# Graph network on one core: the first group's side loads stand ahead of its messages, and these are fetched by SyncE and ScalarE in turn

## The chip, the cores and the metric

The kernel runs on one core of one Trainium2 chip. The metric is the device time in microseconds (us); lower is better. PE is TensorE, DVE is VectorE, ACT is ScalarE, POOL is GpSimd and SP is SyncE. SP computes nothing: it issues DMA transfers and waits. ACT computes, and has a DMA queue of its own as well.

## The reference

Two graph layers act on 6250 nodes of 160 features (64 scalars and 32 vectors of 3) and 100000 edges, sorted by their target. Cut to what matters:

```python
h = relu(layernorm(x))
m = tensor_product(h[dst], edge_attr) + linear(h[dst])     # one message per edge
a = segment_sum(m, src, N)                                 # summed at the nodes
x = x + h + tensor_product(h, a) + linear(h)               # the node update
h = relu(layernorm(x))
m = tensor_product(h[src], edge_attr) * sigmoid(edge_attr16 @ W + b)
x = x + linear(h + segment_sum(m, dst, N))
```

The change lies between the first `segment_sum` and the node update of the first layer, whose tensor product multiplies every pair of features of `h` and `a` by weights.

## The kernel before, in words

There are three stages. **Scatter** makes the messages of the first layer, 128 edges at a time. GpSimd writes each to its place in the DRAM tensor `msgs` (L563), so that messages of 25 neighbouring nodes, a bin, lie together. It also writes the nodes' normalised features to DRAM, in the layouts `hT`, `hX` and `hV`. **Update** sums the messages per node and makes the node update. **Windows** does the second layer.

The update treats the nodes in 13 groups of up to 500. A group has 20 bins, in five *quads* of four bins. For a group it needs:

- the *messages*: `fetch(k)` (L683) loads quad k into a tile `urec`. Each bin is one DMA of 322 KB (128 partitions by 4 rows of 161 floats). Its first row is a value that the device has computed, so that a `value_load` reads it from `start_i` into a register first. There are three `urec` buffers. `sums` (L696) turns a quad into sums: ACT negates the node numbers (`rl`, L706), DVE makes a selection matrix (`uhot`, L711 and L715), PE multiplies (L734), and ACT copies the result (`ag`, L740 and L742). After each quad, the fetch of the quad three further on is called. When all five are done, PE puts the sums into the layout of the products (L755), and ACT copies them into `a` (L751).
- the *sides*: `loads` (L759) brings the group's own features as twelve DMAs: `x0` (L762), `x1` (L764), four for `x1k` (L767), and three each for `x3` and `v3` (L773 and L774).
- `xb` (L815), four DMAs at a time, which POOL multiplies by `a` (L822).

The products follow: PE, DVE and POOL work through a stream of 32 steps per group, `first` and `second`, beginning with the product at L833. While they work on a group, the sums of the next are made between their steps.

The orders of PE, DVE, ACT and POOL are as written (`manual_schedule`). SP's order is laid out by the scheduler of the tile framework: a transfer stands where its buffers and its source allow it, in the order of the calls where they don't decide. `issue_after` keeps the fetches in order. A fetch of `msgs` waits until all of the scatter has landed.

The loads of SP and ACT are told done by eight completion semaphores, which the framework gives out in turn to both queues. An instruction that is given a used one waits for the load that had it before.

Of the kernel before, what the change touches and what calls it, by code (L numbers as in the profile page):

```python
# [36 lines left out]
CAP = 512  # L37
# [19 lines left out]
def gnn_kernel(ctx: ExitStack, tc: tile.TileContext, a: dict, out: bass.AP):  # L57
    nc = tc.nc
# [3 lines left out]
    E = ET * P  # L62
# [16 lines left out]
    msgs = dram.tile([E + CAP, F + 1], F32, name="msgs")  # L79
# [66 lines left out]
    start_i = const.tile([1, NBIN], I32, name="start_i")  # L146
# [143 lines left out]
    def clear(tab):  # L290

        flat = tab.rearrange("(p r) f -> p (r f)", p=P)
        for lo in range(0, flat.shape[1], 400):
            hi = min(lo + 400, flat.shape[1])
            nc.scalar.dma_start(flat[:, lo:hi], zero[:, :hi - lo])
            yield
# [326 lines left out]
    def update():  # L623
# [3 lines left out]
        with ExitStack() as s:  # L627
# [47 lines left out]
            nc.gpsimd.memset(mv, 0.0)  # L675
            eps = wp.tile([P, 1], F32, name="eps")
            nc.gpsimd.memset(eps, EPS)
            last = []

            quads = [(g, q) for g, (_, n) in enumerate(groups) for q in range(0, n // BW, 4)]  # L680
            got = {}

            def fetch(k):  # L683

                if k >= len(quads):
                    return
                g, q = quads[k]
                b0, nq = groups[g][0] // BW + q, min(4, groups[g][1] // BW - q)
                got[g, q] = recs.tile([P, 4, 4, F + 1], F32, name="urec")
                for b in range(nq):  # L690
                    with tc.issue_after(last[-1]) if last else nullcontext():
                        at = nc.sync.value_load(start_i[0:1, b0 + b:b0 + b + 1], min_val=0, max_val=E)
                    last.append(nc.sync.dma_start(got[g, q][:, b], msgs[bass.ds(at, CAP), :]
                                                  .rearrange("(p i) f -> p i f", i=4)).ins)

            def sums(g, a):  # L696

# [29 lines left out]
                for j, (q, nq) in enumerate(qs):  # L727
                    if g == 0 and j + 1 < len(qs):
                        yield from ones(*qs[j + 1])
                    p = pt.tile([P, 4 * P], F32, name="ptr")  # L730
                    rec, hot = got.pop((g, q)), hots.pop(0)
                    for i in range(4):
                        for b in range(nq):
                            nc.tensor.matmul(p[32 * b:32 * b + 32, :F], hot[:, b, i], rec[:, b, i, 0:F],  # L734
                                             start=i == 0, stop=i == 3, tile_position=(0, 32 * b))
                    fetch(quads.index((g, q)) + 3)
                    yield
                    w = 32 * nq
                    ag = pool.tile([P, 4, P], F32, name="ag", bufs=5)
                    nc.scalar.copy(ag[:w, 0].rearrange("p (i f) -> p i f", i=2),  # L740
                                   p[:w, None, 0:M0].to_broadcast([w, 2, M0]))
                    nc.scalar.copy(ag[:w, 1:].rearrange("p k (i f) -> p k i f", i=4),  # L742
                                   p[:w, M0:F].rearrange("p (k f) -> p k f", k=3)[:, :, None]
                                   .to_broadcast([w, 3, 4, M1]))
                    ags.append(ag)
                    if g and j + 1 < len(qs):
                        yield from ones(*qs[j + 1])
                    yield
# [200 lines left out]
            eng = mybir.EngineType  # L949
            with tc.manual_schedule(engines={eng.PE, eng.DVE, eng.Activation, eng.Pool}):  # L950
                R = len(plan)
                stream = [(g, kind, c) for g in range(len(groups)) for kind, c in plan]
                rows = [(i, g, c[1]) for i, (g, kind, c) in enumerate(stream) if kind == "v" and c[0] == 0]
                early = list(rows)
                queue, backs, end = [], [], object()
                clears = itertools.chain(*(clear(t) for t in agg))

                def pop():
                    _, _, grp, item = queue.pop(0)
                    grp.second(*item)  # L960
                    if grp.done():
                        backs.append(grp.back())
                        next(backs[-1])

                for k in range(3):
                    fetch(k)
                gs = {0: Group(0)}
                for _ in gs[0].sums:
                    pass
                for i, (g, kind, c) in enumerate(stream):  # L970
                    r = i % R
                    if r % 8 == 6:
                        next(clears, end)
                    if r == 3 and g + 1 < len(groups):
                        gs[g + 1] = Group(g + 1)
                    while rows and rows[0][0] <= i + 7 and rows[0][1] in gs:
                        gs[rows[0][1]].repeat(rows.pop(0)[2])
                    while early and early[0][0] <= i + 2 and early[0][1] == g:
                        gs[g].ahead(early.pop(0)[2])
                    if r == 2:  # L980
                        while queue and queue[0][2] is not gs[g]:
                            pop()
                    for item in gs[g].first(kind, c):
                        queue.append((g, i + later[kind], gs[g], item))
                    if r == 2:
                        gs[g].begin()
                    queue.sort(key=lambda q: q[:2])
                    while queue and queue[0][1] <= i and queue[0][2].begun:
                        pop()

                    for _ in range((2, 2, 0, 1)[r % 4] if r >= 3 and g + 1 < len(groups) else 0):
                        next(gs[g + 1].sums, end)
                    for _ in range((1, 2, 0, 1)[r % 4]):
                        while backs and next(backs[0], end) is end:
                            backs.pop(0)
                    if r == R - 1 and g + 1 < len(groups):
                        for _ in gs[g + 1].sums:
                            pass
                while queue:
                    pop()  # L1000
                for t in backs + [clears]:
                    for _ in t:
                        pass
# [677 lines left out]
    with tc.tile_pool(name="early", bufs=1) as pool:  # L1681
        e = early(pool)
        update()
        windows(e)
# [93 lines left out]
```

## Time and profile before

The median of three executions is 3754.78 us (3748.99 to 3765.18). The profiled execution took 3762.7 us, with a span of 3760.6 us in the records.

| stretch of the span (us) | what runs | PE busy | DVE busy | POOL busy | clock | DMA share |
|---|---|---|---|---|---|---|
| 0 to 60 | the bins, first tables | 29.29 | 44.64 | 16.16 | 0.86 | 0.61 |
| 60 to 1350 | scatter | 696.26 | 686.03 | 767.42 | 0.70 | 0.53 |
| 1350 to 1412 | from scatter to update | 19.10 | 14.97 | 14.05 | 0.56 | 0.81 |
| 1412 to 2330 | update | 849.65 | 705.16 | 680.41 | 0.99 | 0.54 |
| 2330 to 3761 | windows | 817.34 | 767.70 | 741.26 | 0.63 | 0.47 |

Busy times are in us of the stretch. The clock is the TensorE clock that the throttle granted, as a part of full speed; the DMA share is the mean busy share of the core's 16 DMA engines. In the timelines a line begins with its start and its duration; `SPq` and `ACTq` are transfers issued on the queues of SP and ACT, shown at their issue and not at their landing. `L693` is a line of the kernel.

### The profile page before, as it was taken

The page shows a single profiled execution, that of the slowest core. Times are in us where ns is not written, and L with a number is a line of the kernel's source. Part 1 is how long each engine was busy: PE and PEld are TensorE (multiplying, and loading weights), DVE is VectorE, ACT ScalarE, POOL GpSimd, SP SyncE. Part 2 cuts the span into 40 slices and gives each one's busy share as a digit, 9 for nine tenths or more (in the row PEclk, how much of TensorE's full clock was granted, in tenths as well). Part 3 has the DMA queues.
Part 4 walks back from the last instruction along what each step waited for, and adds up shares of the span by engine and source line. Part 5 has one row for each costly group of instructions (what it writes and reads, how often), then busy time and mean ns, then how long its engine had stood idle before and what let it go on. Part 6 is the DMA issues. An engine that isn't in the chain of part 4 may idle for free. (4 is left out here: it accounts for less than half of the span.)

```text
span 3760.6 us, 47934 instructions
## 1 busy us (share of the span) xinstructions
PE 2411.6 (64%) x12112; PEld 1273.7 (34%) x12112; DVE 2218.5 (59%) x4577; ACT 1547.0 (41%) x5126; POOL 2219.3 (59%) x1864
## 2 busy tenths in 40 slices
PE   5555565565544439999999998455655565655655
PEld 3433343343333323333333333132323333332323
DVE  7665555555444427777777775455555556555554
ACT  4554444554444424544453441333434333433433
POOL 4655555555666537777777775655555555555552
PEclk8677767776666659999999999566666666666666
DMA  6655555555444456665565532445444454445442
GB/s 176 172 162 162 151 160 174 153 171 153 135 132 130 135 178 179 181 181 159 173 182 176 165 116 70 130 131 147 133 136 132 135 141 139 132 134 146 134 132 71
DMA packets 346121, 554.56 MB, mean 147 GB/s; under 512 B 63954, under 2 KB 245168, under 8 KB 339947
## 3 DMA queue, kind: packets, MB, share of 16 engines
q1 hardware_dynamic: 229160, 288.49, 27.7%
q0 software_dynamic: 87584, 218.31, 19.9%
q10 hardware_dynamic: 29091, 44.61, 3.6%
q8 instruction: 99, 1.62, 0.2%
q14 instruction: 187, 1.53, 0.1%
HBM read 418.16 MB, written 133.04 MB: 147 GB/s over the span
## 5 line engine op out<-in xcount | busy, mean ns | idle before, releaser
L563 POOL DMA_INDIRECT msgs<-rec,pos_i x782 | 782.5, 1001 | 568.2 <-issue 223.9
L1060 POOL DMA_INDIRECT wgot<-T,src_i x782 | 741.3, 948 | 636.0 <-issue 423.7
L543 PE MATMUL rank<-seen,every 128*128 128x256 f16 x782 | 261.2, 334 | 449.3 <-ACT junk L556 296.5
L556 ACT ACTIVATE junk<-rank,off 128x256 bf16<-128x256 f32 x782 | 373.2, 477 | 403.5 <-remote 284.5
L545 PE MATMUL pmsg<-tw,d 120*128 120x160 f32 x1564 | 463.4, 387 | 79.8 <-issue 68.8
L1079 PE MATMUL wgate<-wrad,wblk 97*128 97x480 f32 x522 | 378.6, 858 | 175.0 <-issue 133.3
L855 DVE TENSOR_TENSOR pr<-y,a 128x1000 f32<-128x1000 f32 (+1 forms) x312 | 352.7, 1153 | 132.7 <-PE y L852 131.9
L840 POOL TENSOR_TENSOR pr<-pr 128x1500 f32<-128x1500 f32 (+1 forms) x104 | 338.1, 3251 | 149.1 <-DVE pr L837 149.1
L1097 DVE TENSOR_TENSOR whot<-lane,wbank 128x192 f32<-128x192 f32 x131 | 45.9, 350 | 619.4 <-ACT wbank L1205 550.1
L1216 PE MATMUL wbank<-wms,whot 128*32 128x160 f32 x1564 | 255.7, 411 | 213.6 <-ACT wo L1220 104.5
L545 PEld LDWEIGHTS pmsg<-tw,d 120*128 120x128 f32 x1564 | 317.0, 251 | 147.4 <-issue 93.4
L1091 ACT ACTIVATE wm<-wgot,wattr 128x160 f32<-128x160 f32 x782 | 311.1, 398 | 34.9 <-DMA wgot<-T,src_i 12.6
L560 DVE CAST pos_i<-pos 128x4 int32<-128x4 f32 x196 | 42.4, 216 | 419.1 <-ACT junk L556 347.5
L1216 PEld LDWEIGHTS wbank<-wms,whot 128*32 128x32 f32 x1564 | 146.4, 144 | 405.9 <-ACT wo L1220 137.5
L1094 ACT ACTIVATE wsg<-wgate 128x480 f32<-128x480 f32 x259 | 137.5, 566 | 352.7 <-remote 187.7
L860 POOL TENSOR_TENSOR ppr<-ppr,pr 128x1000 f32<-128x1000 f32 (+1 forms) x104 | 232.0, 2231 | 79.5 <-DVE pr L855 77.1
L544 PEld LDWEIGHTS <-upto 128*128 128x128 bf16 x782 | 91.6, 117 | 541.5 <-issue 499.3
L544 PE MATMUL rank<-hot,upto 128*128 128x256 bf16 x782 | 262.2, 335 | 0.5 <-DVE hot L528 0.5
L531 DVE TENSOR_TENSOR seen<-seen,hot 128x256 f16<-128x256 f16 x782 | 230.5, 295 | 45.5 <-DVE hot L528 7.6
L528 DVE TENSOR_SCALAR hot<-binb,qb 128x256 bf16<-128x256 bf16 x782 | 242.7, 310 | 0.0
L1079 PEld LDWEIGHTS wgate<-wrad,wblk 97*128 97x128 f32 x522 | 131.2, 285 | 314.2 <-issue 239.6
L1115 DVE TENSOR_TENSOR wm<-wm,wtb 128x384 f32<-128x384 f32 (+1 forms) x393 | 221.8, 564 | 13.5
(215 smaller groups left out, 4430.2 us busy)
## 6 DMA issues: line engine op xcount, KB each, us to landing
urec<-msgs SPq DMA_DIRECT2D x250, 322.0 KB
attb<-in_attr SPq DMA_DIRECT2D x48, 960.0 KB
tw<-T0s SPq DMA_DIRECT2D x391, 75.0 KB
xb<-hT SPq DMA_DIRECT2D x192, 125.0 KB
dstb<-in_dstrow SPq DMA_DIRECT2D x48, 480.0 KB
T0s<-tt ACTq DMA_DIRECT2D x11, 1200.0 KB
msgs<-rec,pos_i POOLq DMA_INDIRECT x782
wgot<-T,src_i POOLq DMA_INDIRECT x782
```

Of the source, the lines that this page charges most:

```text
L528: nc.vector.tensor_scalar(hot, binb, qb[:, t:t + 1], None, op0=OP.is_equal)
L543: nc.tensor.matmul(rank[:, j % 2], every, before, start=True, stop=False)
L544: nc.tensor.matmul(rank[:, j % 2], upto, hot, start=False, stop=True)
L545: nc.tensor.matmul(prs[-1][:, j % 2, :F], ds[j // WP][:, j % WP], tws[j // WP], start=True, stop=True)
L556: nc.scalar.activation(junk, rank, AF.Relu, bias=off, accum_out=pos[:, j:j + 1])
L563: nc.gpsimd.indirect_dma_start(out=views[(t0 + j) % NV][:, :], out_offset=bass.IndirectOffsetOnAxis(ap=pos_i[:, j:j + 1], axis=0), in_=rec ...
L840: nc.gpsimd.tensor_tensor(prs[0], prs[0], prs[1], op=OP.add)
L855: nc.vector.tensor_tensor(pr[:, :, :n], y[:, :, :n], a[:, j, None, :n].to_broadcast([P, 2, n]), op=OP.mult)
L1060: nc.gpsimd.indirect_dma_start(out=got[u][:, i], out_offset=None, in_=T1[:, :], in_offset=bass.IndirectOffsetOnAxis(ap=src_i[:, t0 + i:t0 ...
L1079: nc.tensor.matmul(p[:, :n], blocks[u // CH][:, u % CH], rad[:, lo * F:lo * F + n], start=True, stop=True)
L1091: nc.scalar.activation(m[:, b, j:j + F], g[:, i, oS1:oS1 + F], AF.Copy, scale=attr(u)[:, i, 0:1])
L1216: nc.tensor.matmul(state["acc"][j:j + WN], hot[:, i], ms[:, i], start=t0 + i == w * WT, stop=t0 + i == end, tile_position=(0, j))
```

## The change

The construction of the first group, which issues its sides, is moved ahead of the first three fetches. And in group 0 the bins of a quad are fetched by SP and ACT in turn: bins 0 and 2 by SP, bins 1 and 3 by ACT, each with a `value_load` on its own engine. Each queue keeps its own order (`last` is now a table by queue). The other groups are fetched by SP alone, as before. Behind the change, line numbers are higher by up to 3.

```diff
-            last = []
+            last = {}
...
                 for b in range(nq):
-                    with tc.issue_after(last[-1]) if last else nullcontext():
-                        at = nc.sync.value_load(start_i[0:1, b0 + b:b0 + b + 1], min_val=0, max_val=E)
-                    last.append(nc.sync.dma_start(got[g, q][:, b], msgs[bass.ds(at, CAP), :]
-                                                  .rearrange("(p i) f -> p i f", i=4)).ins)
+
+                    o = b % 2 if g == 0 else 0
+                    eng = (nc.sync, nc.scalar)[o]
+                    with tc.issue_after(last[o]) if o in last else nullcontext():
+                        at = eng.value_load(start_i[0:1, b0 + b:b0 + b + 1], min_val=0, max_val=E)
+                    last[o] = eng.dma_start(got[g, q][:, b], msgs[bass.ds(at, CAP), :]
+                                            .rearrange("(p i) f -> p i f", i=4)).ins
...
+                gs = {0: Group(0)}
                 for k in range(3):
                     fetch(k)
-                gs = {0: Group(0)}
                 for _ in gs[0].sums:
                     pass
```

## The prediction

> **What bounds the kernel now.** I read first the busy time by stage, to see what a delay at the hand-over from scatter to update is worth. The columns are the stretch in us, its length, busy us of PE, weight loads, DVE, ACT and POOL, the granted clock, the DMA share and GB/s.
>
> ```profile
> 1350.00:1412.00 62.00, 19.10 (x204) 14.49 (x204) 14.97 (x30) 9.36 (x31) 14.05 (x21) 0.56 0.81 242
> 1412.00:2330.00 918.00, 849.65 (x5500) 315.49 (x5498) 705.16 (x680) 390.29 (x1418) 680.41 (x260) 0.99 0.54 158
> ```
>
> From 1412 to 2330 the update keeps PE busy for 849.65 of 918 us at clock 0.99: PE bounds it, and an earlier start of its first product is an earlier end. In the 62 us before, every engine is mostly idle while the DMA share is 0.81: this is the only place that the change touches. Next, the timeline there: start, duration, engine, and in brackets the idle time before and what ended it. ACT's first instruction on each quad (`rl`, L706) waits for the quad's messages:
>
> ```profile
> 1377.74 0.23 ACT L706 ACTIVATE rl<-urec 128x16 f32<-128x16 f32 x1 [23.40 <-DMA urec<-msgs]
> ...
> 1382.49 0.23 ACT L706 ACTIVATE rl<-urec 128x16 f32<-128x16 f32 x1 [4.53 <-DMA urec<-msgs]
> ...
> 1400.68 0.23 ACT L706 ACTIVATE rl<-urec 128x16 f32<-128x16 f32 x1 [3.75 <-DMA urec<-msgs]
> ...
> 1411.19 0.68 PE L833 MATMUL y<-x,w_f 64*128 64x500 f32 x1
> ```
>
> The five quads of group 0 are met at 1377.74, 1382.49, 1388.29, 1396.17 and 1400.68 (the rows of quads 2 and 3, alike, are left out); the first product of the update follows the last by 10.5 us. So the arrival of quad 4 is the number to follow. Third, the issues of SP, one by one:
>
> ```profile
> 1370.32 0.37 SPq L693 DMA_DIRECT2D urec<-msgs  x1
> ...
> 1374.07 0.33 SPq L693 DMA_DIRECT2D urec<-msgs  x1
> ...
> 1383.34 0.89 SPq L767 DMA_DIRECT2D x1k<-hT  x2
> ...
> 1388.13 0.30 SPq L774 DMA_DIRECT2D v<-hV  x1
> 1389.27 0.36 SPq L693 DMA_DIRECT2D urec<-msgs  x1
> ```
>
> The first fetch is issued as soon as the scatter has landed. Twelve stand there, 1.11 us apart; then eight side loads hold SP from 1383.34 to 1389.27, and only after them come the eight fetches of quads 3 and 4. Last, how full the DMA is:
>
> ```profile
> 1370.00:1372.00 2.00, 0.00 (x0) 0.00 (x0) 0.40 (x2) 0.00 (x0) 0.00 (x0) 0.50 0.32 49
> ...
> 1376.00:1378.00 2.00, 0.00 (x0) 0.00 (x0) 0.00 (x0) 0.23 (x1) 0.00 (x0) 0.50 1.00 312
> ...
> 1384.00:1386.00 2.00, 2.00 (x32) 1.34 (x32) 0.00 (x0) 0.00 (x0) 0.00 (x0) 0.50 0.95 305
> ...
> 1388.00:1390.00 2.00, 0.04 (x4) 0.07 (x6) 1.12 (x2) 0.76 (x3) 0.00 (x0) 0.50 0.54 126
> ```
>
> One fetch is 322 KB, 0.330 MB; at 1.11 us that is 297 GB/s, and the rows show 312 and 305 at shares of 1.00 and 0.95 (289 to 304 at about 0.9 in those between). SP's issuing and the DMA are almost equally fast. The holes are at the start (0.32) and where the sides stood (0.54).
>
> **The change, part by part.** *Sides first.* In the built order of SP four of the twelve side loads (x0, x1, two of x1k) already stand ahead of the messages; the change moves the other eight: two x1k of 187.5 KB and six of 62.5 KB, 0.77 MB. What leaves the path: SP's stretch from 1383.34 to 1389.27, less one ordinary 1.11 us step, about 5 us. Where they go: after the x1k issue at 1362.33. The DMA is 0.73 to 0.99 busy there until 1368 with scatter and weights, then 0.37 and 0.32 until 1372, so some 2.6 us of empty DMA hold them; 0.77 MB at 250 GB/s (estimate, between the 205 of 1386 to 1388, where they ran, and 305) is 3.1 us. Left over, or lost by the scatter's tail: 0 to 1 us, taken as 0, since the last of them run beside ACT's first fetch, where the DMA is not yet full.
>
> *What is queued behind them.* SP's and ACT's loads take eight completion semaphores in turn, and an issue waits until the load that last held its semaphore has landed. In the built order one moved x1k thus waits for the second weight load, which landed by 1367.47 (its scaling on DVE starts then), the third x3 waits for w_n, issued at 1367.08, and **the eighth moved load, the last v3, waits for ACT's first fetch to land**. All of SP's own fetches stand behind that v3. So SP cannot begin at 1370.3. ACT does: its first fetch waits for the scatter, 1370.3. Issue to landing is 3.67 us for the fourth fetch before (1374.07 to 1377.74), 3.98 for the eighth, 3.5 for the last two quads; I take 3.5: landing at 1373.8, SP's v3 there, SP's first fetch at 1374.3, four later than now. Ends of this unknown: 3.5, and 4.6 (ACT's 256 KB weight load, 1362.84 to 1367.47 beside others).
>
> *Two queues.* Ten of group 0's twenty fetches go to ACT, six of them ahead of its first `rl`. Each is a register load, a check and a DMA. ACT has nothing else then: its idle time before the first `rl` is 23.4 us, so six times 1.11 us cost nothing; without that cover 6.7. ACT's third fetch reuses the semaphore of its second (issued 1371.5, landed 1375.0). The bytes: two fetches from ACT until about 1373.7, a hole until 1375.3 (SP's issue plus 1 us, as now from 1370.32 to 1371.4), then eighteen fetches with more than enough issuers. A rule is weighed here. The Trainium skill, "DMA: Bandwidth & Descriptors", section "Issuing engines are not separate DMA queues", says that transfers started by different engines interleave on the same 16 DMA engines and that a second issuer only saves issuing time. By it the second queue gives no bandwidth and the eighteen go at the rate of the fullest plain row, 305 GB/s: 1.08 us each, 19.4 us. The same page's table of specifications puts a core's share of HBM at about 358 GB/s: 0.92 us each, 16.6 us. No row here shows fetches above 312, so I take 19.4, and keep 16.6 as an end. 1375.3 + 19.4 = 1394.7, and 1.3 from the last byte to `rl` (3.5 less 1.1 and 1.1): **quad 4 at 1396.0 instead of 1400.68**.
>
> *Do the three buffers allow it?* Quad 3 reuses quad 0's buffer. Quad 0's two halves now share the DMA with others and land about three and a half fetches after 1375.3: 1380.4, 2.7 later than now. Its matmuls end 4.0 later (1377.74 to 1381.79 now): 1384.4. The ten fetches under way last until 1386.1, and new bytes flow 1.1 us after an issue, so the slack is 0.6 us and no hole opens; ACT's half of quad 3 stands behind `rl` of quad 1, which needs only quad 1 (1384.7). For quad 4 the same sum leaves about as little. I allow up to 2 us for holes at the pessimistic end.
>
> *The rest.* ACT loads its first start register during the scatter, at the sixteenth send. The DVE cast it needs ends at 145.76, ACT arrives at 146.4, and ACT idles 2.82 us soon after, waiting for PE: 0 us, at most 1.1 without that cover. POOL's first product needs xb, whose last three loads stay behind group 1's fetches on SP. Now SP comes late: quad 4's matmuls end at 1404.7, xb is issued from 1411.71 and POOL starts at 1417.65. Afterwards these matmuls end at 1400.0; four fetches and three xb on SP take 6.4 us, and 3.3 to land give 1409.7: eight earlier, not a new bound. From the next group on the orders on SP and ACT are the same.
>
> Sum: -4.7 us at quad 4, carried by PE to the end. Ends: with 16.6 us for the fetches -7.5; with 4.6 us to land, 1.14 us per fetch (289 GB/s) and 2 us of holes, 1.1 + 1.1 + 2 given back, -0.5. The profiled execution took 3762.7 (span 3760.6 and 2.1 around it) and becomes 3758.0; that execution stands 7.9 above the median of 3754.8, so I forecast **3750.1**.
>
> **The rivals.** *More than that*: the hold by ACT's first fetch is hidden, because ACT alone fills the DMA for those us, and two queues beat 305 GB/s. Twenty fetches without a hole at 0.92 to 1.0 us from 1371.4, and 1.3, give 1391.1 to 1392.7: 8.0 to 9.6 us less, about 3746. Against it: 1.00 share at 312 GB/s with one queue.
>
> *It does not do what it says*: only eight of twelve loads move, SP is still held by the last of them, and quad 0 lands later by what quad 4 gains. If PE's start then hangs on something else, it is 3755. For it: the 0.6 us of slack; against it: 10.5 us from quad 4 to the first product are pure work on PE and ACT.
>
> *Slower*: the semaphore chain. Place: SP's last v3 behind ACT's first fetch; price: each us by which that fetch lands late delays ten SP fetches, thereby quad 0, its buffer, and quads 3 and 4, one for one once the 0.6 us of slack are gone. It decides when the landing takes 3.5 + 0.6 + 4.7 = 8.8 us; at 12 it gives 3758. Against it: on a quiet DMA the fourth fetch landed after 3.67.
>
> **How the numbers follow.** About 0.5% (18.8 us) is what a measurement of this kernel can tell from no change; the three executions already lie 16 us apart. The forecast (3747 to 3754): 0.63. More: 0.15. Nothing: 0.13. Slower by 1 to 6 us: 0.07. The rest, 0.02, is something unseen. None of the cases reaches 18.8 us either way; only the spread of executions or something unseen does: faster 0.03, same 0.93, slower 0.04. Range: from 3746 of the first rival to 3758 of the last, widened by half the spread of the executions at the lower end and a third at the upper: 3740 to 3762.
>
> **What would show it.** In the trace after: the eight side loads issued between 1362 and 1374; ACT's first fetch near 1370.3 and SP's first some four us behind it; quad 0 later than 1377.74 while quad 4 is earlier, near 1396; the hole at 1388 to 1390 gone; the first product near 1406.5; the update's length unchanged near 918 us. The prediction is wrong if SP's first fetch comes more than 6 us after ACT's, if the bytes stop between quads 2 and 3, or if the update's length takes the gain back.

## The result

The changed kernel takes 3759.02 us (median of 20 runs, 3748.68 to 3773.05), the kernel before 3756.39 us in the same comparison (20 runs, 3743.17 to 3771.61): a ratio of 1.0002, 95% interval 0.9993 to 1.0011, which is no change that can be measured. The forecast was 3750.1 us, in a range of 3740 to 3762. The executions of either kernel lie 24 to 28 us apart, so the 4.7 us that the prediction spoke of do not show in these times, and have to be looked for in the traces, stage by stage. The profiled execution has a span of 3749.6 us (before: 3760.6).

The busy time by stage first, in the changed kernel, for the same two stretches as before (length, busy us of PE, weight loads, DVE, ACT and POOL, clock, DMA share, GB/s):

```profile
1350.00:1412.00 62.00, 24.84 (x213) 16.55 (x213) 20.25 (x32) 10.82 (x38) 15.60 (x19) 0.56 0.79 259
1412.00:2330.00 918.00, 848.88 (x5503) 315.96 (x5501) 699.78 (x681) 389.86 (x1412) 675.12 (x259) 0.99 0.54 158
```

The update is as full as it was: PE 848.88 us of 918 against 849.65, at clock 0.99. The change shows only in the 62 us before it, where more of the work lies ahead of 1412. Next the timeline of the changed kernel there: `rl` of quads 0, 1, 3 and 4, and the first product.

```profile
1377.06 0.23 ACT L709 ACTIVATE rl<-urec 128x16 f32<-128x16 f32 x1 [26.91 <-DMA urec<-msgs]
1380.10 0.23 ACT L709 ACTIVATE rl<-urec 128x16 f32<-128x16 f32 x1 [2.81 <-DMA urec<-msgs]
...
1387.24 0.23 ACT L709 ACTIVATE rl<-urec 128x16 f32<-128x16 f32 x1 [0.98 <-DMA urec<-msgs]
...
1391.95 0.23 ACT L709 ACTIVATE rl<-urec 128x16 f32<-128x16 f32 x1 [3.90 <-DMA urec<-msgs]
...
1403.58 0.68 PE L836 MATMUL y<-x,w_f 64*128 64x500 f32 x1
```

The clock of the trace starts with the execution, so these are to be read from the first fetch, which stood at 1370.32 before and stands at 1365.94 now. Quad 0 comes 11.12 us after it (before 7.42), quad 4 at 26.01 (before 30.36), the first product at 37.64 (before 40.87). The gain is 4.35 us at quad 4 and 3.2 at the first product; 1.1 us are lost between the two. The issues of ACT and SP at the hand-over, in the timeline of the changed kernel:

```profile
1365.94 0.38 ACTq L696 DMA_DIRECT2D urec<-msgs  x1
1369.54 0.30 SPq L777 DMA_DIRECT2D v<-hV  x1
1370.37 0.37 SPq L696 DMA_DIRECT2D urec<-msgs  x1
```

The last moved side load is issued 3.60 us after ACT's first fetch, and SP's own first fetch 4.43 us after it. And the DMA in 2-us stretches of the changed kernel (columns as above):

```profile
1370.00:1372.00 2.00, 0.00 (x0) 0.00 (x0) 0.00 (x0) 0.00 (x0) 0.00 (x0) 0.50 0.38 80
...
1376.00:1378.00 2.00, 0.00 (x0) 0.00 (x0) 0.61 (x1) 0.23 (x1) 0.00 (x0) 0.50 1.03 388
1378.00:1380.00 2.00, 1.25 (x20) 1.12 (x24) 0.50 (x2) 0.00 (x0) 0.00 (x0) 0.50 1.03 402
...
1382.00:1384.00 2.00, 1.93 (x32) 1.02 (x24) 0.42 (x1) 0.78 (x3) 0.00 (x0) 0.50 0.83 200
1384.00:1386.00 2.00, 1.01 (x16) 0.91 (x20) 0.70 (x2) 0.39 (x2) 0.00 (x0) 0.50 1.05 412
```

With two queues the rows reach 388 to 412 GB/s, where one had 312 at the most in the rows shown. (The share adds up the times of the packets that start in a row, so it can pass 1.) But there are two holes, 80 GB/s while SP is held, and 200 GB/s from 1382 to 1384. They take back most of what the fast rows gain.

### The profile page after: what moved, and what is told of

Its sections match the earlier page's. It is cut to its first block, busy times and chain, and to the rows that moved or that the text cites. A ratio compares the mean times of both kernels' runs of the same rounds, so it can differ in the third digit from the quotient of the medians.

```text
span 3749.6 us, 47940 instructions
## 1 busy us (share of the span) xinstructions
PE 2401.2 (64%) x12112; PEld 1270.6 (34%) x12112; DVE 2214.9 (59%) x4577; ACT 1546.4 (41%) x5126; POOL 2215.5 (59%) x1864
## 4 chain that ended last, share of the span: by engine, by line
PE 30%; another core or an unknown queue 22%; DVE 17%; ACT 13%; issue 10%; DMA 5%; SPq 1%; POOL 1%; ACTq 1%; DVEq 0%; POOLq 0%
PE out L871 5%; DVE pr L840 4%; ACT junk L556 3%; ACT wm L1094 3%; PE pmsg L545 3%; PE wbank L1219 3%; PE wgate L1082 2%; PE y L855 2%; PE wbank L1151 2%; PE y L836 2%; DVE wtb L1108 2%; PE rank L544 2%; PE rank L543 2%; DVE wm L1118 1%
## 5 line engine op out<-in xcount | busy, mean ns | idle before, releaser
L1082 PE MATMUL wgate<-wrad,wblk 97*128 97x480 f32 x522 | 370.0, 841 | 178.2 <-issue 137.6
L1118 DVE TENSOR_TENSOR wm<-wm,wtb 128x384 f32<-128x384 f32 (+1 forms) x393 | 221.7, 564 | 13.4
```

Source lines behind the costliest of these rows:

```text
L1082: nc.tensor.matmul(p[:, :n], blocks[u // CH][:, u % CH], rad[:, lo * F:lo * F + n], start=True, stop=True)
L1118: nc.vector.tensor_tensor(mv[:, :, :, 0:M0], mv[:, :, :, 0:M0], tb[:, :nt, k].rearrange("p (b t) w -> p b t w", b=h), op=OP.add)
```

## The experiments

Two theories were set against each other first. *Spread*: 3 to 5 us are gained at the hand-over, and chance in the long stages hides them. *Given back*: a later stage returns them. Each row of the table is one trace, its last column a ratio from all executions. The last scatter write is counted from its issue. Kernels 1 to 4 ran on one chip, 5 to 8 on a second, whose granted clock is higher (mean 0.82 to 0.84 in the traces against 0.75; the kernel before takes 3075.72 us there), 9 to 12 on a third (3724.77 us). Each is compared with the kernel before on its own chip.

| kernel | last scatter write to first fetch | first fetch to quad 0 | to quad 4 | to first product | last scatter write to first product | first product to first gather of the windows | ratio to before (95%) |
|---|---|---|---|---|---|---|---|
| before | 4.79 | 7.42 | 30.36 | 40.87 | 45.7 | 933.5 | |
| changed | 5.33 | 11.12 | 26.01 | 37.64 | 43.0 | 932.8 | 1.0002 (0.9993 to 1.0011) |
| 1 before again | 5.02 | 7.23 | 30.09 | 40.0 | 45.0 | 931.2 | 0.9985 (0.9974 to 0.9996) |
| 2 changed again | 11.00 | 13.16 | 28.93 | 39.3 | 50.3 | 930.9 | 0.9976 (0.9964 to 0.9988) |
| 3 sides only | 5.11 | 7.25 | 25.67 | 35.4 | 40.5 | 930.9 | 0.9990 (0.9977 to 1.0002) |
| 4 queues only | 4.85 | 8.27 | 25.63 | 34.7 | 39.5 | 927.6 | 0.9990 (0.9976 to 1.0004) |
| 5 quad 0 by SP | 2.87 | 10.41 | 26.14 | 35.6 | 38.5 | 930.1 | 0.9988 (0.9980 to 0.9995) |
| 6 late start | 2.71 | 10.02 | 25.98 | 50.1 | 52.8 | 939.4 | 1.0072 (1.0059 to 1.0085) |
| 7 changed, third | 3.65 | 10.99 | 24.98 | 36.7 | 40.4 | 934.9 | 0.9988 (0.9981 to 0.9996) |
| 8 queues, again | 2.65 | 8.36 | 27.13 | 35.6 | 38.2 | 928.6 | 0.9986 (0.9978 to 0.9993) |
| 9 changed, four buffers | 6.34 | 12.13 | 24.45 | 33.4 | 39.8 | 933.0 | 0.9994 (0.9973 to 1.0014) |
| 10 quad 0 by SP, four buffers | 6.24 | 11.54 | 22.75 | 30.7 | 36.9 | 930.0 | 0.9992 (0.9967 to 1.0017) |
| 11 changed, small pools | 11.31 | 12.24 | 26.24 | 36.6 | 47.9 | 927.2 | 0.9981 (0.9961 to 1.0000) |
| 12 before, control | 2.96 | 7.28 | 29.37 | 38.6 | 41.6 | 933.9 | 1.0007 (0.9990 to 1.0024) |

**1 and 2: both kernels once more.** No edit. Expected of the kernel before:

> The kernel before, unchanged, profiled a second time, to learn how far the intervals repeat. Theory A (the hand-over is shorter by about 3 us and this is lost in the spread between executions): from the first fetch to quad 4 30.4 us again within 0.5, quad 4 to the first product 10.5, first product to first gather of the windows 933.5 within 1, while the time up to the first fetch (1370.3) and from the first gather to the end (1415.9) move by 3 us or more. Theory B (the change gives its gain back in the scatter or the windows): those two long parts repeat within 1 us, so that a change of 3 us in them would be an effect. Ratio 1.000.

and of the changed one:

> The changed kernel again. Theory A: first fetch to quad 4 26.0 within 0.5, quad 4 to first product 11.6, first product to first gather 933 within 1; the long parts before and behind come out anywhere within 5 us of the kernel before. Theory B: the scatter or the windows come out longer than in the kernel before by 3 us, in both of its profiles. Ratio by A 0.9990, by B 1.000; the spread of executions of 7 us leaves the ratio alone unable to tell them.

The unchanged kernel measured 3760.48 us and came out at 0.9985 of itself, with an interval that leaves out 1 although nothing was changed; a ratio within 0.15% of 1 therefore says nothing here. The changed kernel measured 3756.48 us, 4.0 under the control beside it, where the first comparison had it 2.6 over. Of the two theories, *spread* is the one that the traces bear out: the first fetch stands at 1370.3 and 1385.3 us in two traces of the same unchanged kernel, and the part from the first gather to the end, 1415.8 and 1412.8 us before, is 1413.1 and 1414.8 us in the changed kernel, so that no later stage is seen to return a gain. The part between them, from the first product to the first gather, was expected to repeat within 1 us and did not: it is 933.5 and 931.2 us before, 932.8 and 930.9 changed.

In the second trace of the changed kernel quad 4 is at 28.93, the worst of the four traces of this hand-over and later than expected; still 1.2 us better than the 30.09 of the control. What was not expected is the row ahead of it: the first fetch comes 11.00 us after the last scatter write. The timeline of this second trace, POOL's last scatter write and ACT's queue:

```profile
1361.34 1.55 POOL L563 DMA_INDIRECT msgs<-rec,pos_i  x1 [0.30 <-issue]
...
1371.18 0.59 ACTq L92 DMA_DIRECT2D w_n<-in_n  x1
1372.34 0.38 ACTq L696 DMA_DIRECT2D urec<-msgs  x1
```

ACT's fetch stands behind seven loads of weights on ACT, and in this execution their issue ends last: the fetch follows the last of them by 1.16 us. SP is late for the same reason. The chain of this trace, of which these are consecutive long pieces, leads from a load for the windows (`wattr`) to a weight on ACT's queue (`w_flu`), which was given the same semaphore, and from there to a side load on SP:

```profile
1363.12 6.28 DMA wattr<-in_attr
1369.42 4.83 DMA w_flu<-in_flu
1374.27 0.30 SPq L777
```

SP's first fetch follows at 1377.12, after four more side loads. ACT's first fetch had landed before the last of these was issued (it took 2.7 to 3.6 us in the traces where a side load did wait for it), so here it held nothing back. Counted from the last scatter write, the first product comes after 50.3 us, against 45.7 and 45.0 in the two traces of the kernel before.

**3 and 4: each part alone.** Sides ahead, all fetches by SP:

```diff
-                    o = b % 2 if g == 0 else 0
+                    o = 0
```

> One part of the change alone: the sides ahead of the messages, all fetches on SP. If the hold of SP behind ScalarE's first fetch costs what I think, this part alone is as good as the whole change: no hold, first SP fetch as soon as the scatter has landed, twenty fetches at 1.11 us, quad 4 at 1.11 x 19 + 0.5 + 3.5 = 25.1 us after the first fetch (whole change 26.0, before 30.4). If the two queues carry the gain instead, quad 4 stays near 28 or later. Ratio 0.9987 by the first, 0.9995 by the second.

Two queues, the sides left where they were:

```diff
-                gs = {0: Group(0)}
                 for k in range(3):
                     fetch(k)
+                gs = {0: Group(0)}
```

> The other part alone: fetches in turn on SP and ScalarE, the eight sides still behind the first three quads on SP. No hold of SP's first fetch. If two queues move the messages faster than 305 GB/s, quad 0 lands 5.5 to 6.5 us after the first fetch (before 7.4), quad 2 about 13 (18.0), and the sides still delay SP's half of quads 3 and 4: quad 4 at 25 to 27. If the second queue brings nothing, quad 4 at 29 to 30. Ratio 0.9988 by the first, 0.9998 by the second.

Each part alone brings quad 4 to the same place as both together (25.67, 25.63, and 26.01 or 28.93), and the first product earlier than both together: 35.4 and 34.7 against 37.6 and 39.3. The parts don't add up. With the sides alone, the fetches leave SP almost without a pause, the first sixteen within 17.41 us, and quad 4 is bound by issuing (25.1 us expected). With the queues alone quad 4 came as expected, but quad 0 at 8.27 us (5.5 to 6.5 expected) and quad 2 at 17.39 (about 13). The times, 3758.75 and 3759.81 us, lie with the control's.

A part of the 2 to 3 us by which the single changes lead goes with PE's clock. The layout matmuls between quad 4 and the first product (L758), in the changed kernel and then with the sides alone (min/median/max ns, first and last start):

```profile
L758 PE MATMUL ptr<-quad,ag x40: 275/421/536, 1395.9 to 1403.4; 128*128 128x100 f32 x40
```

```profile
L758 PE MATMUL ptr<-quad,ag x40: 275/275/536, 1400.3 to 1405.8; 128*128 128x100 f32 x40
```

The same forty matmuls take a median of 421 ns in one and 275 in the other, and 7.5 against 5.5 us from the first to the last. In the changed kernel the granted clock stands at 0.50 until 36 us after the first fetch; with the sides alone it is at 1.00 from 32 us on. What raises it earlier was not tried, so the cause is open.

**5: without the hold.** Quad 0 by SP alone; in this built order no side load waits for a fetch of ACT.

```diff
-                    o = b % 2 if g == 0 else 0
+                    o = b % 2 if g == 0 and q else 0
```

> The changed kernel, but quad 0 is fetched by SP alone; quads 1 to 4 alternate as before. No side load then stands behind a fetch of ACT, so the hold of SP is gone. Theory A (the hold of SP's last v3 is what eats the second queue's gain: 4.4 and 4.8 us in the two traces of the changed kernel, whose quad 0 came 11.1 and 13.2 us after the first fetch against 7.2 to 7.4 before): SP's first fetch comes at or before ACT's, quad 0 7.3 to 8.8 us after the first fetch, quad 4 at 22 to 24 instead of 26.0 and 28.9, the first product at 32 to 34 instead of 37.7 and 39.3. Theory B (the DMA itself is full, so that any order of the twenty fetches ends alike, as the sides alone with 25.7 and the queues alone with 25.6 suggest): quad 4 at 25 to 26 whatever quad 0 does. From the first product to the first gather of the windows 928 to 933 us under both. Time: A about 5 us under the changed kernel of this call, ratio to it 0.9987; B no difference.

The hold is gone, as the timeline of this kernel shows:

```profile
1090.58 0.37 SPq L696 DMA_DIRECT2D urec<-msgs  x1
1090.64 0.38 ACTq L696 DMA_DIRECT2D urec<-msgs  x1
```

but quad 0 comes at 10.41 (7.3 to 8.8 expected) and quad 4 at 26.14 (22 to 24 expected). SP issues quad 0's four fetches by 3.64 us, but by 4.40 ACT has issued four of quads 1 and 2, and all of them share the DMA. The theory that the hold eats the second queue's gain fell. Theory B had the number right, but not the reason: the DMA isn't full, as its 2-us stretches in this kernel show.

```profile
1100.58:1102.58 2.00, 0.00 (x0) 0.00 (x0) 1.12 (x2) 0.23 (x1) 0.00 (x0) 0.50 1.04 408
1102.58:1104.58 2.00, 1.90 (x32) 1.63 (x36) 1.12 (x2) 0.23 (x1) 0.00 (x0) 0.50 0.42 120
1104.58:1106.58 2.00, 1.81 (x40) 1.35 (x32) 0.00 (x0) 0.00 (x0) 0.00 (x0) 0.79 0.18 43
```

Twelve fetches fill three buffers at up to 408 GB/s, and are done before PE (1.90 and 1.81 us busy in those rows) has emptied the first. A third theory follows: with two queues, the three buffers set quad 4's arrival. The trace of the changed kernel shows the wait itself, in the 32 matmuls of quad 0 and the next fetch of each queue:

```profile
1378.74 2.36 PE L737 MATMUL ptr<-urec,uhot 128*32 128x160 f32 x32 [30.61 <-DVE uhot L718]
1381.25 0.33 SPq L696 DMA_DIRECT2D urec<-msgs  x1
1381.28 0.36 ACTq L696 DMA_DIRECT2D urec<-msgs  x1
```

The fetches before these were issued at 1376.26 and 1374.10. Then neither queue issues one until quad 0's matmuls end at 1381.10; both go on within 0.2 us of that. With the sides alone it is not so: there quad 0's matmuls end 11.30 us after the first fetch, and SP comes to quad 3 only at 14.09.

**6: a shift of known size.** To see what a microsecond at the hand-over is worth, group 0's four copies of the gathered sums were each written thirteen times.

```diff
-                        nc.scalar.copy(a[:, j - 1, :n], p[:, :n])
+                        for _ in range(13 if g == 0 else 1):
+                            nc.scalar.copy(a[:, j - 1, :n], p[:, :n])
```

> The changed kernel with the copy of group 0's gathered sums (ACT, four of them, 0.58 us each) written thirteen times instead of once: 48 copies more, 27.8 us, ahead of the first product, and nothing else. Theory A (PE bounds the update, so whatever happens at the hand-over is carried to the end one for one): the first product 60 to 68 us after the first fetch, first product to first gather still 928 to 933 us, the end 24 to 30 us later, ratio to before 1.0064 to 1.0080. Theory B (the update has room that takes a shift of the hand-over back): first product to gather shorter by 10 us or more, ratio under 1.004.

3097.41 us (5 runs): 24.6 more than the changed kernel beside it (3072.81), 21.7 more than before, ratio 1.0072. Of 27.8 us added on ACT, 88% reach the end by the medians. In the two traces it is less: the first product comes 13.4 us later than in experiment 7's, not 23 or more, and the first gather 17.9 us later, counted from the first fetch. The first product did not wait for all four blocks: PE stood 6.84 and 5.31 us for the copies of the first two, and the others ran beside the products (939.4 us to the first gather, where 928 to 933 was expected). So the theory that the update takes a shift back fell, since of the 13.4 us nothing was returned; that each microsecond is carried through exactly is not shown.

**7 and 8: changed, and queues only, for another trace.** No edit beside those above.

> The changed kernel once more, for its trace. In its first trace the first fetch (ACT's) was issued 5.3 us after the last scatter write was, in its second 11.0, where ACT's weight loads, which stand ahead of it, ended only 1.2 us before. Theory A (chance of the execution: the weights are done in time in most executions): 4.8 to 5.5 us, quad 4 26 to 29 us after the first fetch, first product 37.5 to 39.5. Theory B (the moved sides slow the weights on the shared queues and semaphores as a rule): 8 us or more again, so that the gain at the hand-over is gone when it is counted from the last scatter write (45.0 and 45.7 us to the first product before the change). Time: within 0.15% of before under A (a gain of 2 to 4 us), 1.0000 to 1.0015 under B.

> The two queues without the moved sides once more, for its trace. Theory A (each part alone is worth 5 to 6 us at the hand-over, both together less, because the sides stand on SP between ACT's first fetch and SP's): SP's and ACT's first fetches within 0.3 us of each other, quad 4 25 to 27 us after the first fetch, first product 34 to 36, 39 to 41 us after the last scatter write. Theory B (the first trace was a lucky one): quad 4 at 28 or later. Time: 4 to 6 us under before by the hand-over, ratio 0.9984 to 0.9990, if the other stages average out.

On this chip the executions of a kernel lie 9 to 17 us apart. The changed kernel takes 3072.81 us against 3075.72 (54 runs), 2.9 less; the queues alone 3070.95, 4.8 less; experiment 5 is 3.9 less. First fetch, quad 4 and first product of the changed kernel are where theory A put them, a little better (3.65, 24.98, 36.7). It does not settle the late first fetch, however: on this chip ACT's last weight load was issued 17 to 20 us ahead of the first fetch in all four traces, in the other ten 1.2 to 7.4 us. In the queues alone quad 4 came at 27.13 (25 to 27 expected), the first product at 35.6 as expected, 38.2 after the last scatter write (39 to 41 expected).

**9 to 12: the buffers.** A fourth buffer for the messages, and fetches one quad further ahead; for room the product pools lose one buffer each. Experiment 9 does this to the changed kernel, experiment 10 to that of experiment 5.

```diff
-            recs = s.enter_context(tc.tile_pool(name="ur", bufs=3))
+            recs = s.enter_context(tc.tile_pool(name="ur", bufs=4))
-            prod = s.enter_context(tc.tile_pool(name="prod", bufs=4))
-            pair = s.enter_context(tc.tile_pool(name="pair", bufs=5))
+            prod = s.enter_context(tc.tile_pool(name="prod", bufs=3))
+            pair = s.enter_context(tc.tile_pool(name="pair", bufs=4))
...
-                    fetch(quads.index((g, q)) + 3)
+                    fetch(quads.index((g, q)) + 4)
...
-                for k in range(3):
+                for k in range(4):
```

> The changed kernel with four buffers for the messages of a quad instead of three, and the fetches one quad further ahead; to make room the pools of the update's products have one buffer less each (pair 5 to 4, prod 4 to 3). Theory C (the three buffers set the arrival of quad 4: with quad 0's buffer free only some 4 us after its `rl`, the DMA runs dry, 190 to 228 GB/s in the changed kernel's traces at 14 to 18 us after the first fetch): no such dip, quad 4 at 21 to 24 us after the first fetch instead of 25.0 to 28.9. Theory D (twenty fetches simply take 25 us of DMA): quad 4 at 25 or later. First product under C 32 to 36 us after the first fetch, under D 36 to 39. Time: C 2 to 4 us under the changed kernel with the smaller pools, D the same as that one.

> Quad 0 by SP alone (no hold by ACT's first fetch) together with the fourth buffer, pools of the products one less each. With three buffers this order left the DMA at 120 and 43 GB/s from 12 to 16 us after the first fetch, and quad 4 came at 26.1. Theory C (buffers): no dip, twenty fetches at some 390 GB/s (0.85 us each) from 1.1 us on and 1.3 to the `rl`: quad 4 at 19.5 to 21.5, first product 29 to 33 instead of 35.6. Theory D (DMA): quad 4 at 25 to 26, first product 35 to 36. Time: C 4 to 6 us under the changed kernel with the smaller pools, D the same.

Experiment 11 has the smaller pools alone (the lines of `prod` and `pair`), experiment 12 is the kernel before.

> The changed kernel with the smaller pools of products alone (pair 4, prod 3, three message buffers): what the room for the fourth buffer costs. Theory A (PE bounds the update, the products run ahead of it): first product to first gather 928 to 935 us as before, time within 0.15% of the changed kernel. Theory B (the pools set how far DVE and POOL run ahead): 5 us or more longer. At the hand-over: quad 4 25 to 29 us after the first fetch, the first product 36.5 to 39.5, a fourth trace of it.

> The unchanged kernel, to see what the order of runs alone makes of a ratio: in the first set it came out at 0.9985 of itself. Ratio 0.9985 to 1.0015; a ratio of 0.998 or less for another kernel of this set is then more than the order of runs can give. In its trace quad 4 30 to 30.5 us after the first fetch, the first product 40 to 41, first product to first gather 931 to 934.

Quad 4 comes at 24.45 (21 to 24 expected) instead of 26.24 (experiment 11, same chip), and without the hold at 22.75 instead of 26.14 (experiment 5, another chip); the first product at 33.4 and 30.7 instead of 36.6 and 35.6. The 24.45 alone would prove little, since with three buffers the four traces of the changed hand-over lie between 24.98 and 28.93. But the 22.75 is below all of them, and the wait has moved: with four buffers it is quad 4 that takes quad 0's, and its first fetches are issued within 0.2 us of the end of quad 0's matmuls, 16.34 us (matmuls 16.19) and 15.75 us (15.59) after the first fetch. So the buffers are the bound, as theory C had it, and with the fourth they still are, which is why the 19.5 to 21.5 us of experiment 10 were not reached. The 2-us stretches of experiment 10 show what is left:

```profile
1371.87:1373.87 2.00, 0.77 (x13) 0.68 (x17) 1.30 (x3) 0.23 (x1) 0.00 (x0) 0.50 1.06 402
1373.87:1375.87 2.00, 2.00 (x36) 1.70 (x32) 0.81 (x2) 0.00 (x0) 0.00 (x0) 0.50 0.97 344
1375.87:1377.87 2.00, 1.72 (x28) 0.98 (x20) 0.00 (x0) 0.77 (x4) 0.00 (x0) 0.50 0.85 208
```

One dip to 208 GB/s is left where there were two rows of 120 and 43. In the times none of it shows: 3721.31 and 3722.21 us against 3725.64 of the control, and 3715.22 with the smaller pools alone, which has the later hand-over and the lowest time, where theory C had expected the fourth buffer 2 to 6 us under it. With twelve runs each and 13 to 29 us between the executions of one kernel, these intervals are 0.3 to 0.5% wide. The smaller pools cost nothing that can be seen. Whether they gain anything is open, as is whether the 3 to 6 us of the fourth buffer reach the end. In the control quad 4 (29.37) and the first product (38.6) came some 1 us earlier than expected.

Experiment 11 is also the fourth trace of the changed hand-over, and repeats what experiment 2 had shown: 11.31 us from the last scatter write to the first fetch, which comes 1.16 us after ACT's last weight load (1341.68, 1342.84). In experiments 9 and 10 the first fetch is not behind the weights, and still comes 6.3 and 6.2 us after the last scatter write, against 2.96 in the control on that chip: there the write itself took 5.9 and 5.8 us to land, in the control 2.6. Moved side loads were under way beside it; whether they are the reason was not tried.

## Why the prediction was right, and where not

The forecast of no measurable change held. The path was right as well: SP is held, quad 0 comes later, quad 4 earlier, and PE goes on as before. The size, 4.35 us at quad 4 for 4.7 predicted, is in part luck, since two steps were wrong and cancel, and it is counted from a first fetch that can itself be late. Step by step:

- *SP held by ACT's first fetch.* Right in the profiled trace, and nearly in size: the last v3 3.60 us after that fetch (3.5 predicted), SP's first fetch 4.43 (4.0). In experiment 7 the same chain gives 3.75. In experiments 2 and 11 SP comes as late (4.78 and 5.25), but held by weights on ACT's queue, whose semaphores the side loads take over too.
- *The second queue gives no bandwidth.* Wrong. The share of 1.00 at 312 GB/s was read as a full DMA; two queues moved 388 to 412 at shares of 1.03 to 1.05. The cap was SP's issuing: one fetch in 1.11 us, and SP still takes 1.11 to 1.13 us for each while ACT issues beside it. The Trainium skill, "DMA: Bandwidth & Descriptors", section "Issuing engines are not separate DMA queues", grants a second issuer the saving of issuing time, and this was such a case; the page's 358 GB/s, kept as the other end, was passed as well. The trace of the kernel before already had a row above both figures, 10 to 12 us ahead of the first fetch, with the scatter and loads of both queues on the DMA at once:

```profile
1358.00:1360.00 2.00, 0.00 (x0) 0.00 (x0) 1.66 (x4) 0.00 (x0) 1.69 (x2) 0.50 1.04 384
```

- *No hole between the quads, 0.6 us of slack.* Wrong. Quad 0 came 3.7 us later (2.7 predicted), so its buffer came free later, while the faster queues used the others up sooner: 200 GB/s from 1382 to 1384. This took back what the faster queues gave; the traces and experiments 5, 9 and 10 show the buffers as the bound. Two errors of opposite sign made the sum right. The prediction had named a stop of the bytes between quads 2 and 3 as a sign of being wrong. In the profiled trace they only slow down; in experiment 2 they all but stop, 16 us after the first fetch:

```profile
1388.34:1390.34 2.00, 1.22 (x20) 0.57 (x12) 0.86 (x2) 0.23 (x1) 0.00 (x0) 0.50 0.10 33
```

- *The side loads cost nothing ahead of the fetches.* Open. The prediction listed what is queued behind SP's sides, but not what stands ahead of ACT's first fetch on ACT. In experiments 2 and 11 this fetch was issued behind ACT's late weights, 11.0 and 11.3 us after the last scatter write, against 3.0 to 5.0 in three traces of the kernel before, where SP's fetches don't stand behind these loads. What the weights had waited for, `wattr` (6.28 and 7.48 us to land), was issued before the first moved side load in both, so the moved sides did not begin the delay; whether they lengthened it, or the landing of the scatter, was not separated.
- *10.5 us from quad 4 to the first product, unchanged.* Off by about 1: 11.6, 10.3, 11.7 and 10.3 in four traces, against 10.5, 9.9 and 9.2 before. The work is the same, at the clock that is granted.
- *POOL's first product some 8 us earlier.* It started 40.8 us after the first fetch instead of 47.3, 6.5 earlier, and bounded nothing.
- *Carried to the end by PE.* It fits: 932.8 us against 933.5 to the first gather, and a shift that was not returned in experiment 6. But this stretch lies between 927.2 and 934.9 us over the traces with no added copies, which is more than the gain.

That leaves the sum. From the first fetch, the first product comes 3.2, 0.7 and 2.0 us earlier than in the kernel before in three pairs of traces, where 4.7 was forecast (the third is experiment 11, with its smaller pools, against 12). From the last scatter write, it comes 2.7 us earlier in the first pair, and 5.3 and 6.3 us later in the other two. Only in the pair in which ACT's fetch was not late is the gain left, so whether the change gains anything at the hand-over as a rule is open. The medians show +2.6, -4.0 (against the control) and -2.9 us in three comparisons. They fit a gain of about 3 us, and none as well: a control alone moved by 0.15%, 5.6 us. Of the rivals, "more" had the rate right (388 to 412 GB/s), but not the buffers; "nothing" put quad 0's lateness in the right place; "slower" had the wrong place: the last v3 followed ACT's first fetch by 2.9 to 4.3 us in the four traces, never 8.8, but in two of them that fetch itself was late.

## What to carry to other kernels

When a stream of loads feeds a ring of buffers, work out three limits, the issuing, the bytes and the return of the buffers: here an unbroken single stream brought quad 4 at 25.7 us and two streams at 25.0 to 28.9, by different limits, and only a fourth buffer brought less (24.45 and 22.75). When a first load moves to another engine's queue, list what stands ahead of it there as well as what stands behind it. And when a change is worth a thousandth, measure the unchanged kernel as a candidate of its own beside it, and judge by intervals between events in the trace, counted from an event ahead of the change, here the last scatter write.

## What the runs showed that was not expected

- A DMA share of 1.00 is no ceiling: where SP alone fetched, the full rows stood at about 270 to 317 GB/s with shares of 0.86 to 1.00; two queues reached 388 to 412 with 1.03 to 1.05. The packets of the fetches, 2576 bytes each, took 131 ns in the mean in the row of 312 GB/s and 104 ns in that of 412. Why they were slower with one queue is open.
- In thirteen of the fourteen traces (all but experiment 6) the granted clock rose from 0.50 to 1.00 at 25 to 39 us after the first fetch, ahead of the first product, and fell back to about 0.50 some 7 to 10 us later. The forty layout matmuls took 7.5 us where it rose late and 5.5 where it rose early, in the two traces shown.
- The granted clock differs between chips: a mean of 0.745 and 0.823 for the same kernel, 3756.5 and 3072.8 us.
